# Tokens of each L1 run placed in four groups of two tiles instead of two groups of four, the slots of two groups computed together

## The chip, the cores and the metric

The kernel runs on one core of a Trainium2 chip. A core has engines that each work through their own instruction stream in order: TensorE (PE; the loading of its weights is listed as PEld), VectorE (DVE), ScalarE (ACT), GpSimd (POOL) and SyncE (SP, which here only starts DMAs). They wait for one another by semaphores. The metric is the device time of one execution in microseconds; the median of three runs counts.

## The reference

Two sequences of 1024 tokens with 256 features pass through six layers with residual sums. Everything is float32.

```python
x = x + 0.5 * _L0_ffn_ref(_layernorm(x), ...)     # MoE: 8 experts, top 2, width 176
x = x + _L0_attn_ref(_layernorm(x), ...)          # time mix and channel mix
x = x + 0.5 * _L0_ffn_ref(_layernorm(x), ...)
x = x + 0.5 * _L1_ffn_ref(_layernorm(x), ...)     # MoE: 32 experts, top 6, width 96
x = x + _L1_attn_ref(_layernorm(x), ...)          # linear attention: one sum over a sequence
x = x + 0.5 * _L1_ffn_ref(_layernorm(x), ...)
return x
```

The L1 mixture of experts takes a sigmoid of `x @ gate_w`, keeps the six highest of 32 scores, divides them by their sum, and adds up, with these weights, `silu(x @ wg[e]) * (x @ wu[e]) @ wd[e]` of the six experts; a shared expert of width 192 is added for every token. The attention's sum A runs over all tokens of one sequence, so its output exists only when all tokens of that sequence have been through it.

## The kernel before

The 2048 tokens are 16 tiles of 128, and they stay in SBUF as `x[0]` to `x[15]`. A mixture of experts is computed sparsely (`sparse_moe`): each pair of a token and a chosen expert gets a slot, a row of a DRAM tensor `xs`, so that blocks of 128 slots belong to one expert each. The steps of one such run are these.

- `prep`: normalize four tiles, transpose them, multiply with the router (`lg`), choose the experts (`route`: `taken` and the weights `comb`).
- `plan`: number the pairs. `count` sums up how many pairs each expert has, `cum` how many blocks it has opened, `rank` is a pair's place among its expert's pairs, and `far` holds, broadcast over the partitions, where an expert's blocks begin. From these come the slots and their six indices per token (`idx`). Blocks are numbered group by group: the tokens of a group fill the block that their expert has open, and then blocks opened for this group.
- `scatter`: one indirect DMA of GpSimd for each tile and each of the six choices writes the normalized rows to their slots in `xs` (line 566).
- `owners` finds which expert owns each block (`ends`, `passed`, `who`), `weights` the six factors of each token.
- `blocks`: for each block load 128 slots (`fetch`), transpose them (`px`), multiply with the gate and up weights of the block's expert (`pg`, L764), form the product `h` (L650), transpose it (`ph`), multiply with the down weights (`py`, L781), copy the result to `yb` (L789, VectorE) and store it to the DRAM tensor `ys`. An L1 run has 68 blocks that are always computed; 11 more lie behind a condition (`tc.If`, L906) that TensorE, VectorE, ScalarE and SyncE have to pass, and that borrow one buffer of the gathers.
- `gather` and `add_back` (`combine`): one indirect DMA of GpSimd for each tile and choice fetches result rows from `ys` (L801), and VectorE adds them, weighted, to `x` (L813). There are eight buffers `yk`, used in a ring.
- `shared`: the shared expert, tile by tile.

L1 has four such runs. Both sequences (A: tiles 0 to 7, B: tiles 8 to 15) go through the L1 mixture twice, with the attention between: 0A and 0B are the first passes, 1A and 1B the second (`m1` and `m2` in the code). The profile writes their names as L_0A, L_0B, L_1A and L_1B (xs_A, ys_A belong to both runs of A). The order on the chip is: blocks of 0A, blocks of 0B with the attention of A (`at`) between them, shared parts and the attention of B, blocks of 1A, blocks of 1B, and last the shared part of 1B with its gathers. Each run has two groups of four tiles, so 24 scatters and 24 gathers a group, 96 transfers a run.

A gather may read any block that can hold a pair of its group, so it waits for the stores of the first `first[g]` blocks, a bound that holds for any choice of experts:

```python
first = [moe_blocks(w, BT * (g + 1)) for g in range(NB)]   # L1: 55 and 79
```

The order of the work is made in two steps. While the program is written, a `Clock` with estimated costs (1.41 us for an L1 block, 1.27 us for a GpSimd call, 1.4 us for a pause) runs threads beside the main line of blocks: `between`, `first_pass`, `second_pass`, `sends` and `given_rows`. A thread waits for a condition (`0 in ready1[0]`), yields the time at which it wants to go on, and adds with `clock.spent` what its work costs the main line. A group's gathers begin when the main line has come to block `first[g]` + 3. After every third call on GpSimd stand five small memsets, a pause of the queue; in the last part pauses are off. Then a scheduler orders the instructions of each engine by a timeline of its own. The result is a fixed order on every engine: an instruction that waits holds all that stand behind it on its engine.

Of the kernel before, what the change touches and what calls it, by code (L numbers as in the profile page):

```python
# [8 lines left out]
F32 = mybir.dt.float32  # L9
I32 = mybir.dt.int32  # L10
AF = mybir.ActivationFunctionType
ALU = mybir.AluOpType
# [43 lines left out]
def macaron_kernel(ctx: ExitStack, tc: tile.TileContext, a: dict, out: bass.AP):  # L56
# [35 lines left out]

    before128 = const.tile([P, 32], F32, name="before128")
# [72 lines left out]
    def route(w, lg, name, taken=None, comb=None):  # L166
# [6 lines left out]
        s = small.tile([P, BT, S], F32, tag="s", name=f"s_{name}")  # L173
        nc.vector.memset(s, -1.0)
        sc = s[:, :, 0:E]
        if K == 2:
            mx = small.tile([P, BT], F32, tag="mx", name=f"mx_{name}")
            nc.vector.tensor_reduce(mx, lg, AX.X, ALU.max)
            nc.vector.tensor_tensor(
                sc, lg, mx.unsqueeze(2).to_broadcast([P, BT, E]), ALU.subtract  # L180
            )
            nc.scalar.activation(sc, sc, AF.Exp)
            tot = small.tile([P, BT], F32, tag="tot", name=f"tot_{name}")
# [3 lines left out]
                sc, sc, tot.unsqueeze(2).to_broadcast([P, BT, E]), ALU.mult  # L187
# [3 lines left out]
        m8 = small.tile([P, BT, 8], F32, tag="m8", name=f"m8_{name}")  # L191
        for i in range(BT):
            nc.vector.max(m8[:, i, :], s[:, i, 0:E])
# [3 lines left out]
        rest = small.tile([P, BT, S], F32, tag="rest", name=f"rest_{name}")  # L197
        for i in range(BT):
            nc.vector.match_replace(rest[:, i, :], m8[:, i, :], s[:, i, :], -2.0)
        if taken is None:  # L200
            taken = small.tile([P, BT, E], F32, tag="taken", name=f"taken_{name}")
        nc.vector.tensor_scalar(taken, rest[:, :, 0:E], -1.5, None, ALU.is_lt)
        if comb is None:
            comb = small.tile([P, BT, E], F32, tag="comb", name=f"comb_{name}")
# [3 lines left out]
        else:  # L208
            tot = small.tile([P, BT], F32, tag="tot", name=f"tot_{name}")
# [4 lines left out]
                comb, comb, tot.unsqueeze(2).to_broadcast([P, BT, E]), ALU.mult  # L214
# [180 lines left out]
    HT = NT // 2  # L395
    QK = 3
# [3 lines left out]
    def sparse_moe(layer, w, name, x, xs, ys, moe, given=None, out=None, bufs=2):  # L400
# [6 lines left out]
        NB = NT // BT  # L407
        NBLK, sure = moe_blocks(w, NT), SURE[layer]

        first = [moe_blocks(w, BT * (g + 1)) for g in range(NB)]  # L410
# [32 lines left out]
        def prep(b):  # L443
            sub = f"{name}_{b}"
            ts = slice(BT * b, BT * b + BT)
            xb, xbT, o = places(BT * b)
            xb = [xb[:, o + i, :] for i in range(BT)]
            sent[b] = xb
            features_of(b, xb, xbT, o, sub)
            lg = bank("pt", f"lg_{sub}")[:, 0 : BT * E].rearrange("p (t e) -> p t e", e=E)  # L450
            for i in range(BT):
                for c in range(DC):
                    nc.tensor.matmul(
                        lg[:, i, :],
                        xbT[:, c, (o + i) * P : (o + i + 1) * P],
# [4 lines left out]
            route(w, lg, sub, taken[:, ts, :], comb[:, ts, :])  # L460

        def plan(g):


            sub = f"{name}_{g}"
            lo, hi = BT * g, BT * g + BT
            pc = bank("pt", f"count_{sub}")
            for t in range(lo, hi):
                nc.tensor.matmul(
                    pc[0:E, 0:1], taken[:, t, :], ones, start=(t == lo), stop=(t == hi - 1)  # L470
                )


            count = small.tile([E, 1], F32, tag="count", name=f"count_{sub}", bufs=2)
            if g == 0:
                nc.vector.tensor_copy(count, pc[0:E, 0:1])
            else:
                nc.vector.tensor_tensor(count, pc[0:E, 0:1], groups[-1]["count"], ALU.add)
            over = small.tile([E, hi], F32, tag="over", name=f"over_{sub}")
            nc.vector.tensor_scalar(over, steps128[0:E, 0:hi], count, None, ALU.is_lt)  # L480
            cum = small.tile([E, 1], F32, tag="cum", name=f"cum_{sub}", bufs=5)
            nc.vector.tensor_reduce(cum, over, AX.X, ALU.add)
            own = cum
            if g > 0:
# [51 lines left out]
            else:  # L536

                def wide(v):
                    return v.unsqueeze(1).to_broadcast([P, BT, E])
# [1031 lines left out]
```

## Time and profile before

| | us |
|---|---|
| median of three runs | 1432.81 (1429.22 to 1433.11) |
| the profiled execution | 1429.86 |
| its span, first to last instruction | 1428.0 |
| TensorE busy | 1255.6 |
| GpSimd busy | 667.6 |

The span is read in stages. From the timelines: L0 lies before about 700; the blocks of 0A run from 731 to 855, those of 0B to 1041, those of 1A from 1156 to 1270, those of 1B to 1372. GpSimd's transfers lie as follows.

| GpSimd | from | to | number |
|---|---|---|---|
| scatters of 0A | 626.8 | 717.1 | 24 + 24, gathers of L0 between |
| scatters of 0B | 731.7 | 809.3 | 48 |
| gathers of 0A | 838.4 | 935.9 | 48 |
| gathers of 0B | 983.0 | 1093.8 | 24 + 24, 12 scatters of 1A between |
| scatters of 1A | 1021.1 | 1152.0 | 12 + 36 |
| scatters of 1B | 1152.3 | 1229.6 | 48 |
| gathers of 1A | 1251.8 | 1342.4 | 48 |
| gathers of 1B | 1354.4 | 1420.0 | 48 |

A view of waits names, for each instruction that began late, the engine and line whose semaphore came last. A timeline lists instructions with their start, their length and, in brackets, how long their engine stood idle before them and what ended that.

### The profile page before, as it was taken

What the parts mean: (1) busy time and instruction counts of PE and PEld (TensorE: products, weight loads), DVE (VectorE), ACT (ScalarE), POOL (GpSimd) and SP (SyncE); (2) the same over time, 40 slices, a digit from 0 to 9 for tenths busy, and PEclk for the clock granted to TensorE, in tenths of its full rate; (3) what the DMA queues carried; (4) which work ended last, traced back from release to release, by engine and by line L of the source; (5) the groups of instructions that cost most, each with busy time, mean ns of one, the idle gap of its engine ahead of it and who ended that gap; (6) DMA issues with size and microseconds to landing.
All of it is one profiled execution on the core that took longest, in us unless ns stands there. A gap on an engine that the chain in (4) does not pass through costs nothing. (4 is left out here: it accounts for less than half of the span.)

```text
span 1428.0 us, 23152 instructions
## 1 busy us (share of the span) xinstructions
PE 1255.6 (88%) x6100; PEld 973.0 (68%) x6100; DVE 737.3 (52%) x2507; ACT 631.9 (44%) x1671; POOL 667.6 (47%) x1346
## 2 busy tenths in 40 slices
PE   6599889889999789989979999988888789999970
PEld 4577657456666667757658987776665578988850
DVE  4433444865552432455536446665577446456653
ACT  4023562487674323362434555453333235555520
POOL 1640532010111460267777537413767777366475
PEclk8589889889999769989968999999879779999995
DMA  9723422990000922433476778443322247778843
GB/s 284 240 76 107 137 82 65 318 310 22 0 0 14 233 86 88 135 110 116 142 222 211 248 216 239 124 146 91 112 67 71 82 161 254 229 231 261 247 138 104
DMA packets 195170, 214.94 MB, mean 151 GB/s; under 512 B 40892, under 2 KB 178012, under 8 KB 195036
## 3 DMA queue, kind: packets, MB, share of 16 engines
q1 hardware_dynamic: 170460, 146.22, 33.2%
q0 software_dynamic: 24576, 67.14, 15.5%
q8 instruction: 59, 0.97, 0.3%
q14 instruction: 75, 0.61, 0.2%
HBM read 103.04 MB, written 110.23 MB: 149 GB/s over the span
## 5 line engine op out<-in xcount | busy, mean ns | idle before, releaser
L801 POOL DMA_INDIRECT yk_L<-ys_L,idx_L x64 | 62.1, 971 | 185.4 <-DMA ys_L<-yb_L 122.5
L333 POOL MEMSET still<- 128x96 f32 x628 | 112.7, 179 | 35.9
L764 PE MATMUL pg_L_b<-L0gu,xbT_L 128*128 x312 | 110.3, 479 | 0.0
L566 POOL DMA_INDIRECT xs_L<-xn_L,idx_L x64 | 61.9, 967 | 74.0 <-DVE idx_L L557 36.4
L659 PE MATMUL pg_L<-L0sgu,xTs_L 128*128 128x352 f32 x256 | 91.9, 495 | 2.8 <-DVE h_L L650 2.8
L801 POOL DMA_INDIRECT yk_L_0B<-ys_B,idx_L_0B x48 | 48.8, 1017 | 72.0 <-DMA ys_B<-yb_L_0B 47.0
L781 PE MATMUL py_L_b<-L0down,hT_L_b 88*128 x312 | 81.4, 383 | 0.0
L801 POOL DMA_INDIRECT yk_L_0A<-ys_A,idx_L_0A x48 | 46.6, 970 | 61.9 <-DMA xb_L_0A<-xs_A 29.2
L781 PEld LDWEIGHTS py_L_b<-L0down,hT_L_b 88*128 88x128 f32 x312 | 59.3, 193 | 19.7 <-issue 0.7
L764 PEld LDWEIGHTS pg_L_b<-L0gu,xbT_L 128*128 128x128 f32 x312 | 56.5, 199 | 20.1 <-issue 3.0
L650 DVE TENSOR_TENSOR h_L_b<-g_L_b,pg_L_b 128x176 f32<-128x176 f32 x78 | 26.2, 336 | 83.6 <-ACT g_L_b L649 73.7
L801 POOL DMA_INDIRECT yk_L_1A<-ys_A,idx_L_1A x48 | 46.3, 964 | 48.5 <-DMA xb_L_1A<-xs_A 22.2
L659 PEld LDWEIGHTS pg_L<-L0sgu,xTs_L 128*128 128x128 f32 x256 | 49.0, 204 | 27.0 <-DVE h_L L650 5.0
L983 PE MATMUL pkk_cm<-mk_cm,w_WkeyT 128*128 128x512 f32 x128 | 62.6, 621 | 4.9 <-DVE mk_cm L975 3.2
L764 PE MATMUL pg_L_0A_b<-L1gu,xbT_L_0A 128*128 x272 | 60.0, 347 | 1.8 <-DVE shift_L_0B L135 0.9
L764 PE MATMUL pg_L_0B_b<-L1gu,xbT_L_0B 128*128 x272 | 60.7, 350 | 0.8 <-DVEq L906 0.8
L801 POOL DMA_INDIRECT yk_L_1B<-ys_B,idx_L_1B x48 | 45.8, 954 | 27.2 <-DMA ys_B<-yb_L_1B 12.0
L995 PE MATMUL pkv_cm<-w_WvalT,sk_cm 128*128 128x256 f32 x256 | 58.0, 380 | 0.1
L764 PE MATMUL pg_L_1B_b<-L1gu,xbT_L_1B 128*128 x272 | 56.3, 329 | 1.6 <-DVEq L906 1.6
L764 PE MATMUL pg_L_1A_b<-L1gu,xbT_L_1A 128*128 x272 | 57.2, 334 | 0.5 <-DVE m_L_1B L194 0.4
L649 ACT ACTIVATE g_L_b<-pg_L_b 128x176 f32<-128x176 f32 x78 | 24.7, 317 | 72.6 <-PE pg_L_b L764 69.3
L995 PEld LDWEIGHTS pkv_cm<-w_WvalT,sk_cm 128*128 128x128 f32 x256 | 48.3, 190 | 12.0 <-issue 5.0
(639 smaller groups left out, 3387.5 us busy)
## 6 DMA issues: line engine op xcount, KB each, us to landing
xs_A<-zero SPq DMA_DIRECT2D x1, 10112.0 KB
xs_B<-zero SPq DMA_DIRECT2D x1, 10112.0 KB
xb_L<-xs_L SPq DMA_DIRECT2D x78, 128.0 KB
ys_L<-yb_L SPq DMA_DIRECT2D x78, 128.0 KB
xb_L_0A<-xs_A SPq DMA_DIRECT2D x68, 128.0 KB
ys_A<-yb_L_0A SPq DMA_DIRECT2D x68, 128.0 KB
xb_L_0B<-xs_B SPq DMA_DIRECT2D x68, 128.0 KB
ys_B<-yb_L_0B SPq DMA_DIRECT2D x68, 128.0 KB
```

The costliest lines, as they stand in the source:

```text
L333: d = nc.gpsimd.memset(still, 0.0)
L566: d = nc.gpsimd.indirect_dma_start(out=xs, out_offset=bass.IndirectOffsetOnAxis(ap=idx[:, t, k : k + 1], axis=0), in_=sent[g][t - BT * g], ...
L649: nc.scalar.activation(g, pg[:, 0:width], AF.Silu)
L650: nc.vector.tensor_tensor(dst, g, pg[:, width : 2 * width], ALU.mult)
L659: nc.tensor.matmul(pg, xbT[:, c, i * P : (i + 1) * P], w["sgu"][:, c, u, :, :].rearrange("p z w -> p (z w)"), start=(c == 0), stop=(c == D ...
L764: nc.tensor.matmul(pg, xbT[:, c, :], w["gu"][:, c, bass.ds(e, 1), :, :].rearrange("p e z h -> p (e z h)"), start=(c == 0), stop=(c == DC - 1),
L781: mm = nc.tensor.matmul(py, hT[0:HP, k, :], w["down"][:, bass.ds(e, 1), k, :].rearrange("p e d -> p (e d)"), start=(k == 0), stop=(k == C ...
L801: d = nc.gpsimd.indirect_dma_start(out=yk, out_offset=None, in_=ys[0 : n * P, :], in_offset=bass.IndirectOffsetOnAxis(ap=idx[:, t, k : k + ...
L983: nc.tensor.matmul(ps, w[:, c, oc * P : (oc + 1) * P], src[:, c, :], start=(c == 0), stop=(c == DC - 1),)
L995: nc.tensor.matmul(ps, src[:, c, i * P : (i + 1) * P], w[:, c, :], start=(c == 0), stop=(c == n - 1),)
```

## The change

The number of tiles in a group becomes a parameter `GT` of `sparse_moe`: four for L0 as before, two (`FINE`) for L1. An L1 run then has four groups, and `first` is 43, 55, 67 and 79. Slots are still planned for four tiles at a time, that is for two groups at once (`plan(g0, g1)`), so the same number of plans is made, but each has terms for two groups: the counts of both come from one chain of matmuls against shifted columns of a constant `ramp` (zeros and then ones), `cum` has a column for the state before, `far` has up to six parts instead of up to three, a pair that lies past the first group's open block gets a first shift and one past the second's a second (`more`), and the blocks left open (`open`) are worked out behind the indices. `owners` works with four group ends instead of two. Gathers, scatters and the threads count four groups; the attention starts when both groups of its four tiles have been added; the estimated cost of a plan goes from 3.5 (7.0) to 4.5 (8.0). The tiles `s`, `m8`, `rest` of `route` and `over` have one buffer instead of two.

```diff
+    ramp = const.tile([P, 2, BT], F32, name="ramp")
+    nc.gpsimd.memset(ramp[:, 0, :], 0.0)
+    nc.gpsimd.memset(ramp[:, 1, :], 1.0)
...
+    FINE = 2
...
-        first = [moe_blocks(w, BT * (g + 1)) for g in range(NB)]
+        first = [moe_blocks(w, GT * (g + 1)) for g in range(NG)]
...
-        def plan(g):
+        def plan(g0, g1):
...
             for t in range(lo, hi):
+                j = (t - lo) // GT
                 nc.tensor.matmul(
-                    pc[0:E, 0:1], taken[:, t, :], ones, start=(t == lo), stop=(t == hi - 1)
+                    pc[0:E, 0:G],
+                    taken[:, t, :],
+                    ramp[:, BT - j : BT - j + G],
+                    start=(t == lo),
+                    stop=(t == hi - 1),
                 )
...
+            cum = small.tile([E, 1 + G], F32, tag="cum", name=f"cum_{sub}", bufs=5)
+            if was is None:
+                nc.vector.memset(cum[:, 0:1], 0.0)
+            else:
+                nc.vector.tensor_copy(cum[:, 0:1], was["cum"])
+            nc.vector.tensor_reduce(cum[:, 1 : G + 1], over, AX.X, ALU.add)
+            own = small.tile([E, G], F32, tag="own", name=f"own_{sub}", bufs=2)
+            nc.vector.tensor_tensor(own, cum[:, 1 : G + 1], cum[:, 0:G], ALU.subtract)
...
+            shift0 = [(col(own, 0), before128)] if was is None else []
+            sums = [
+                ([(col(cum, j), others128)] if g0 + j else []) + [(col(own, j), before128)]
+                for j in range(G)
+            ]
+            sums += [[(col(cum, j), own128)] + shift0 for j in range(G) if g0 + j]
+            last = g1 == NG
+            if not last:
+                sums += [[(col(own, j), ident)] for j in range(G) if g0 + j]
...
+                for j in range(G - a):
+                    more = sl
+                    if j:
+                        more = small.tile([P, n, E], F32, tag="s", name=f"more_{sub}_{j}", bufs=1)
+                    nc.vector.tensor_tensor(more, pr, wide(far[:, G + j, :]), ALU.is_ge)
+                    nc.vector.tensor_tensor(more, more, wide(step[:, j, :]), ALU.mult)
+                    if j:
+                        nc.vector.tensor_tensor(sl, sl, more, ALU.add)
...
+            if not last:
+                for j in range(G - a):
+                    gone = small.tile([P, E], F32, tag="open", name=f"open_{sub}_{j}", bufs=2)
+                    nc.vector.tensor_tensor(gone, far[:, j + a, :], open_, ALU.subtract)
+                    nc.vector.scalar_tensor_tensor(
+                        gone, far[:, 2 * G - a + j, :], 0.5, gone, ALU.is_gt, ALU.mult
+                    )
+                    nc.vector.tensor_tensor(gone, gone, open_, ALU.add)
+                    open_ = gone
...
-            n = first[t // BT]
+            n = first[t // GT]
...
         for g in range(TPB // BT):
-            yield from wait(lambda: g in added)
+            yield from wait(lambda: {2 * g, 2 * g + 1} <= added)
...
+        n = m["groups"] // 2
         with behind_blocks():
-            m["plan"](g)
-        yield clock.spent(3.5, 7.0)
-        planned.add(g)
+            m["plan"](n * g, n * g + n)
+        yield clock.spent(4.5, 8.0)
+        planned.update(range(n * g, n * g + n))
...
     def sends(m, planned, sent, h, rank):
-        for g in range(2):
+        for g in range(BT):
             yield from wait(lambda: g in planned[h])
             yield from m[h]["scatter"](g, rank)
             sent[h].add(g)
```

In the fixed order that results, GpSimd has, between the gathers of run 0A and the last scatters of 1A: 24 gathers of 0B, 12 scatters of 1A, 12 gathers of 0B, 3 scatters, 12 gathers, 33 scatters. Before it had 23 gathers, 2 scatters, 1 gather, 10 scatters, 24 gathers, 36 scatters. Each L1 run has 42 matmuls instead of 29 in its counts, ranks, `far`, `ends` and `owners`, and 52 VectorE operations instead of 34 in its plans and owners.

## The prediction

> **What bounds the kernel now.** I read the page first, then the chain that ended last, TensorE's and GpSimd's busy time by stage, GpSimd's waits, and the timelines around those waits. On the page TensorE is the busiest engine:
>
> ```profile
> span 1428.0 us, 23152 instructions
> PE 1255.6 (88%) x6100; PEld 973.0 (68%) x6100; DVE 737.3 (52%) x2507; ACT 631.9 (44%) x1671; POOL 667.6 (47%) x1346
> ```
>
> But the shares hide stages with other limits. The busy time by stage (columns: stretch, its length, then PE, PEld, DVE, ACT, POOL busy, granted clock, DMA share, GB/s):
>
> ```profile
> 945.00:1045.00 100.00, 83.88 (x382) 66.30 (x383) 56.12 (x209) 40.05 (x104) 45.23 (x91) 0.83 0.30 95
> 1100.00:1165.00 65.00, 52.05 (x223) 41.27 (x222) 29.02 (x104) 20.07 (x45) 51.58 (x111) 0.74 0.30 103
> 1165.00:1260.00 95.00, 94.56 (x608) 85.53 (x608) 49.98 (x187) 50.39 (x192) 57.85 (x121) 1.00 0.73 232
> 1385.00:1428.00 43.00, 0.37 (x2) 0.00 (x0) 15.62 (x33) 0.00 (x0) 26.62 (x28) 0.55 0.37 107
> ```
>
> The expert blocks (1165 to 1260) are TensorE's: 94.56 of 95 us. The last 43 us are not: TensorE has nothing left, and the chain that ended last goes through GpSimd's gathers of run 1B, 1.25 us apart, to the last add. So in the tail the time at which the gathers begin decides. What they wait for (engine, line, releaser: us in all, times, longest):
>
> ```profile
> POOL yk_L_0B L801 <- DMA ys_B<-yb_L_0B: 47.0, 1, 47.0
> POOL yk_L_0A L801 <- DMA xb_L_0A<-xs_A: 29.2, 1, 29.2
> POOL yk_L_1A L801 <- DMA xb_L_1A<-xs_A: 22.2, 1, 22.2
> POOL yk_L_1B L801 <- DMA ys_B<-yb_L_1B: 12.0, 1, 12.0
> ```
>
> Once in each of the four L1 runs GpSimd stands idle until block 54 is stored. In the tail, on GpSimd's timeline:
>
> ```profile
> 1341.49 0.95 POOL L801 DMA_INDIRECT yk_L_1A<-ys_A,idx_L_1A  x1 [0.52 <-DVE h_L_1B_b L650]
> 1354.42 0.94 POOL L801 DMA_INDIRECT yk_L_1B<-ys_B,idx_L_1B  x1 [11.97 <-DMA ys_B<-yb_L_1B]
> ...
> 1419.03 0.94 POOL L801 DMA_INDIRECT yk_L_1B<-ys_B,idx_L_1B  x1 [0.30 <-DVE x L813]
> ```
>
> From 1354.42 on nothing holds it: 48 gathers, the first 11 in the paced rhythm (three, then five memsets, 5.1 us), the rest 1.25 us apart.
>
> In the middle, blocks of run 1A start when the last scatter of xs_A (1151.08 to 1152.04) has landed; on TensorE's timeline:
>
> ```profile
> 1149.69 2.39 PE L995 MATMUL po_at<-wA_at,axT_at 128*128 128x256 f32 x8
> 1155.84 1.12 PE L742 MATMUL px_L_1A<-ident,xb_L_1A 128*128 128x128 f32 x4 [3.76 <-DMA xb_L_1A<-xs_A]
> ```
>
> **The change, part by part.**
>
> *When gathers may start.* A group's gathers wait for as many blocks as can at most hold its pairs: (tiles x 768 + 4064)/128, now 43, 55, 67, 79 (before: 55 and 79). So 12 of 48 gathers may start after block 42 instead of 54.
>
> *The tail.* Copies of block results: block 42 ends at 1333.9, block 54 at 1350.5, and the first gather came 3.9 us after the latter. So run 1B's gathers start at 1337.8, if run 1A's are over: these also start 17 us earlier (1231.7 against 1248.7 for block 42 and 54 of 1A) and ended at 1342.4, so at about 1331 even with another 6 us of stalls. In the changed order of GpSimd five pauses lie in the first 15 gathers (before: four in the first 11). A pause adds 1.36 us to a gather's step. The 22nd gather would start at 1337.8 + 21 x 1.25 + 5 x 1.36 = 1370.9, but it takes a buffer that the conditional blocks (L906) hold until TensorE passes them (before it was the 19th):
>
> ```profile
> 1377.87 1.53 PE L659 MATMUL pg_L_1B<-L1sgu,axT_at 128*128 128x384 f32 x4 [0.81 <-DVEq L906]
> ```
>
> That place in TensorE's order is the same after the change. So the 22nd gather starts at 1378.2 and the 48th 26 x 1.25 later, 1410.7 instead of 1419.03: **-8.3**. Bounds: if the buffer comes free earlier, 1370.9 + 32.5 = 1403.4, -15.6; if the gathers hold the blocks up, half of it. I take the gate, since in run 1A the gather with that buffer stood 1.51 us until TensorE had passed.
>
> *More work for the slots.* Counted in the two instruction orders, a run gets 13 more small matmuls on TensorE (7 of L518, 4 of L590, 2 of L610) and 18 more operations on VectorE. From TensorE's timeline four L518 take 0.9 us (0.23 each), two L590 0.14, an L610 0.3: 7 x 0.23 + 4 x 0.07 + 2 x 0.3 = 2.5 us a run. VectorE: 0.07 to 0.47 us (L543 to L548, L605), 0.25 on average, 4.5 us a run; its share in those stages is at most 81% (44.57 of 55), and it costs only where TensorE waits for it. Run 0A and half of 0B lie beside the L0 blocks, where TensorE has few gaps (1.3 and 0.9 us) and the load of L1's down weights (702) waits for its end: 2.5 (0 to 3.7). The second half of 0B lies beside 0A's blocks: 1.4. So 0B's blocks start **+3.9** late (0 to 5). The second half of 1B beside 1A's blocks: 1.4; two output matmuls (po_at, 0.95 each) now stand behind 1A's first blocks, where they no longer fill the wait of 3.76: 1.0 (0 to 1.9). **+2.4**. L0's runs: one or two tiny operations more a group (0.07 to 0.15), while the update of the open blocks (0.3) moves behind idx: from -0.9 to +0.6, taken as 0. The scratch of route is single now, but all its users stand in one order on VectorE: 0 (to +1).
>
> *The middle.* The orders of VectorE and TensorE move attention A ahead: its first normalization from block 20 of run 0B to block 11, the second from 45 to 37, its output, 1A's router and slots in front of block 66. I walk along VectorE by the distances of before (without the 3.9). First normalization 889.5 -> 873.5; fourth tile 917.4 -> 901.4; 17 blocks of 1.49: second normalization 947.6 -> 933; block 42 stored 943, so gather 1 at 947 (before 983). Output and normalization for 1A 1001 -> 986; block 54 at 1000 (before 980), because pA, four po and the router now precede it. The second dozen of gathers runs 1004 to 1024; before they ran on by themselves. Their add-backs stand on VectorE in front of block 61's gate product and 1A's second normalization: 1021 + 3.9 = 1025. Behind these lie the router, the slots and blocks 61 to 66: block 66 copied at 1043 (before 1030.6), the last at 1048 (1041.2). GpSimd: 12 scatters 1024 to 1043, then the third dozen of gathers, which stands in front of all other scatters and waits for block 66: 1047 to 1067; 3 scatters to 1072; the last dozen to 1092; 33 scatters of 1.61 to 1145, with 3 us of stalls 1148 instead of 1152: **-4.0**. The bounds are wide: -12 if block 66 comes at 1038 and nothing stalls (before, the same 24 gathers took 2.03 each), +8 if block 66 comes 10 us later or add-backs stall as before.
>
> *Sum:* 1429.9 (the profiled execution; span 1428.0) + 3.9 - 4.0 + 2.4 - 8.3 = 1423.9. The median shown is 1432.81, 2.95 above it, so about **1427** for the median.
>
> [...] The row first: before 1A's first transposes TensorE stood 5.81 us, with only output matmuls ahead of it, and the granted clock was 0.83 in that stage; at the second such place shared matmuls stood between and the gap was 3.66. After the change the second place is bare too: by the rows 2.15 us more, which the walk along VectorE contains. [...]
>
> **The rivals.** (1) *More than that:* the buffer's gate doesn't bind in the tail. For it: before, the 19th gather had 0.30 us of idle time, no wait. Against: run 1A's 1.51. Tail -15.6 instead of -8.3: 1420 by the median, and with the middle's good end (-12) 1412. (2) *Slower:* one mechanism, in the middle: the third dozen of 0B's gathers stands in GpSimd's one queue in front of 1A's remaining scatters, and block 66 is late because attention's work is in front of it and its add-backs wait for the second dozen. Each us of lateness past 1047 passes to the start of 1A's blocks. It decides when the third dozen starts after about 1057: then +6 instead of -4 and 1437; at 1062, 1442. For it: the wait of 47.0 shows that these gathers hang on the blocks, and they are issued in order. Against: GpSimd has 26 us of slack before (from about 921 to 947) and a dozen done early. (3) *No change:* TensorE pays all of the extra matmuls (+7.3), the middle gives nothing and the tail -8.3: 1432. (4) *The change doesn't do what it says,* if GpSimd isn't free when block 42 is stored; in the tail it is, about 6 us before.
>
> **How the numbers follow.** Forecast 1427, own range 1421 to 1433: 0.42. Rival 1 (1412 to 1420): 0.24. Rival 2 (1437 to 1442): 0.20. Rival 3 (1430 to 1436): 0.14; rival 4 is under 0.01. A measurement tells about 0.3% (4.3 us) from no change, so faster means below 1428.5: 0.24 + 0.33 of the forecast's = 0.57. Slower means above 1437.1: 0.20 with rival 2's upper part and what I have not seen. The rest, 0.23, within. The range reaches from rival 1's good end to rival 2's middle: 1413 to 1439.
>
> **What would show it.** Run 1B's first gather at about 1338 minus the shift of the start, the 22nd held until TensorE passes L906's place, the last about 8 us sooner after that; run 0B's gathers in four dozens with a stop before the second (until block 54) and before the third (until block 66); xs_A's last scatter a few us sooner than 1152. The prediction is wrong if the third dozen starts far from 1047 + 4, or if the tail's gathers run without a stop.

## The result, and the profile after

The changed kernel took 1449.26 us (median, 1448.80 to 1457.41) beside 1431.01 us (1425.51 to 1433.11) of the kernel before, four runs of each: a ratio of 1.0144, 95% interval 1.0111 to 1.0178. The prediction was 1427, range 1413 to 1439, most likely faster. It was wrong in sign, and the time lies above the range.

The page of the changed kernel has 19 us more span, and TensorE is busy for 12 us more of it:

```profile
span 1447.0 us, 23428 instructions
PE 1267.9 (88%) x6200; PEld 985.2 (68%) x6200; DVE 751.0 (52%) x2593; ACT 625.1 (43%) x1667; POOL 667.3 (46%) x1353
```

The next view is the busy time by stage, in stretches shifted so that they lie at the same work as those shown of before (stretch, its length, PE, PEld, DVE, ACT, POOL, granted clock, DMA share, GB/s):

```profile
957.00:1057.00 100.00, 87.07 (x448) 69.64 (x447) 59.37 (x232) 37.65 (x104) 45.84 (x96) 0.83 0.33 102
1112.00:1177.00 65.00, 48.82 (x193) 38.20 (x194) 28.03 (x105) 13.90 (x34) 42.91 (x89) 0.66 0.24 83
1178.00:1273.00 95.00, 92.01 (x574) 82.29 (x574) 50.19 (x192) 49.01 (x172) 67.53 (x144) 0.95 0.70 219
1404.00:1447.00 43.00, 7.20 (x30) 5.00 (x30) 17.77 (x39) 1.56 (x5) 26.65 (x28) 0.63 0.37 107
```

In the second row, the stretch up to 1A's first blocks, the granted clock fell from 0.74 to 0.66 and GpSimd was busy for 42.91 us instead of 51.58. In the third, 1A's first blocks, it is 0.95 instead of 1.00. In the last row TensorE still has 7.20 us of work where before it had 0.37: the tail is now shorter than 43 us.

From the timelines of the two profiled executions, the sum of the change stage by stage ("block 0 of 0A" is the copy of its result on VectorE):

| stage | before | after | difference |
|---|---|---|---|
| start to L0's second scatters | 478.8 | 481.0 | +2.2 |
| to block 0 of 0A | 276.5 | 282.2 | +5.7 |
| to block 0 of 0B | 99.3 | 101.5 | +2.2 |
| to block 42 of 0B | 87.3 | 90.3 | +3.0 |
| to the last scatter of 1A | 210.1 | 209.2 | -0.9 |
| to block 0 of 1A | 16.2 | 17.5 | +1.3 |
| to block 15 of 1A | 25.2 | 38.6 | **+13.4** |
| to the last block of 1B | 178.5 | 177.1 | -1.4 |
| to the last gather of 1B | 48.1 | 41.6 | **-6.5** |
| sum | 1420.0 | 1439.0 | +19.0 |

The tail gave about what was forecast. The largest loss stands in a place to which the prediction gave 2.4 us: the first fifteen blocks of 1A. TensorE's timeline there, in the changed kernel:

```profile
1159.42 2.05 PE L1045 MATMUL po_at<-wA_at,axT_at 128*128 128x256 f32 x4
1167.91 0.69 PE L790 MATMUL px_L_1A<-ident,xb_L_1A 128*128 128x128 f32 x2 [6.43 <-DMA xb_L_1A<-xs_A]
1168.53 0.79 PE L531 MATMUL rank_L_1B<-before,own_L_1B 32*128 32x128 f32 x2
...
1171.11 0.61 PE L552 MATMUL far_L_1B<-ident,own_L_1B 32*128 32x32 f32 x2
...
1172.13 1.91 PE L1045 MATMUL po_at<-wA_at,axT_at 128*128 128x256 f32 x4
...
1176.97 1.89 PE L1045 MATMUL po_at<-wA_at,axT_at 128*128 128x256 f32 x8
...
1186.42 1.54 PE L161 MATMUL pt_L_1B<-ident,axl_at 128*128 128x128 f32 x8 [2.03 <-DVE axl_at L152]
1188.43 3.68 PE L461 MATMUL lg_L_1B<-L1router,axT_at 128*128 128x32 f32 x16 [0.46 <-ACT axT_at L443]
```

The same place in the kernel before, where the transposes of block 0 come at 1155.84:

```profile
1146.83 0.79 PE L502 MATMUL rank_L_1B<-before,cum_L_1B 32*128 32x128 f32 x2
1147.42 0.47 PE L518 MATMUL far_L_1B<-before,cum_L_1B 32*128 32x32 f32 x2
1147.82 4.26 PE L995 MATMUL po_at<-wA_at,axT_at 128*128 128x256 f32 x12
...
1163.41 1.87 PE L453 MATMUL lg_L_1B<-L1router,axT_at 128*128 128x32 f32 x16
```

(In these rows each matmul of the kernel counts twice, a transpose once: the router's x16 are eight matmuls, the x12 of `po_at` the outputs of three tiles.)

In the changed kernel the transposes of 1A's block 0 (L790) wait 6.43 us for the last scatter of 1A, and now the last part of `rank` and all of `far` of 1B's first plan, and the outputs of three of the four remaining tiles (`po_at`), stand behind them. Before, all of these stood in front. So work that was ready filled nothing, and 1B's slots came late. The rows of the next normalization, which need those outputs, came late too, and TensorE waits a second time for them (2.03 us). VectorE waits for `far`, and GpSimd for the indices (VectorE's timeline, then GpSimd's):

```profile
1171.76 0.29 DVE L561 COPY far_L_1B<-far_L_1B 128x128 f32<-128x128 f32 x1 [9.76 <-PE far_L_1B L552]
...
1174.49 0.17 DVE L593 TENSOR_SCALAR idx_L_1B<-top_L_1B 128x24 int32<-128x24 f32 x1
```

```profile
1163.24 0.96 POOL L614 DMA_INDIRECT xs_A<-axl_at,idx_L_1A  x1 [0.30 <-issue]
...
1174.93 0.96 POOL L614 DMA_INDIRECT xs_B<-axl_at,idx_L_1B  x1 [9.59 <-DVE idx_L_1B L593]
```

Before, on VectorE's timeline, 1B's indices were written two microseconds ahead of 1A's last scatter (1151.08):

```profile
1148.79 0.18 DVE L557 TENSOR_SCALAR idx_L_1B<-top_L_1B 128x24 int32<-128x24 f32 x1
```

In the tail, GpSimd's timeline shows the earlier start and a stop:

```profile
1363.64 0.94 POOL L849 DMA_INDIRECT yk_L_1B<-ys_B,idx_L_1B  x1 [3.72 <-DMA xb_L_1B<-xs_B]
...
1392.94 0.95 POOL L849 DMA_INDIRECT yk_L_1B<-ys_B,idx_L_1B  x1 [0.30 <-DVE h_L_1B L698]
1402.71 1.06 POOL L849 DMA_INDIRECT yk_L_1B<-ys_B,idx_L_1B  x1 [8.82 <-DVE x L861]
...
1438.01 0.94 POOL L849 DMA_INDIRECT yk_L_1B<-ys_B,idx_L_1B  x1 [0.30 <-DVE x L861]
```

19 gathers run, the twentieth stands for 8.82 us until an add-back of VectorE (L861) has been done, and the last 29 run 1.25 us apart.

### The profile page after: what moved, and what is told of

Read it like the earlier page. It is cut to its first block, busy times and chain, and to the rows that moved or that the text cites. A ratio compares the mean times of both kernels' runs of the same rounds, so it can differ in the third digit from the quotient of the medians.

```text
span 1447.0 us, 23428 instructions
## 1 busy us (share of the span) xinstructions
PE 1267.9 (88%) x6200; PEld 985.2 (68%) x6200; DVE 751.0 (52%) x2593; ACT 625.1 (43%) x1667; POOL 667.3 (46%) x1353
## 5 line engine op out<-in xcount | busy, mean ns | idle before, releaser
L698 DVE TENSOR_TENSOR h_L_b<-g_L_b,pg_L_b 128x176 f32<-128x176 f32 x78 | 26.2, 336 | 86.8 <-ACT g_L_b L697 74.2
L707 PEld LDWEIGHTS pg_L<-L0sgu,xTs_L 128*128 128x128 f32 x256 | 47.7, 199 | 25.2 <-DVE h_L L698 4.4
L614 POOL DMA_INDIRECT xs_B<-axl_at,idx_L_1B x48 | 46.6, 971 | 23.6 <-issue 11.9
```

Of the source, the lines that this page charges most:

```text
L614: d = nc.gpsimd.indirect_dma_start(out=xs, out_offset=bass.IndirectOffsetOnAxis(ap=idx[:, t, k : k + 1], axis=0), in_=sent[t], in_offset=None,
L698: nc.vector.tensor_tensor(dst, g, pg[:, width : 2 * width], ALU.mult)
L707: nc.tensor.matmul(pg, xbT[:, c, i * P : (i + 1) * P], w["sgu"][:, c, u, :, :].rearrange("p z w -> p (z w)"), start=(c == 0), stop=(c == D ...
```

## The experiments

The theory after the result: the order of TensorE at 1A's head costs most of it. The rivals: GpSimd's line of gathers in front of 1A's scatters (the prediction's rival 2), and the longer slot computation itself. The kernel before took between 1427 and 1458 us on different chips and at different times, so kernels are compared by their ratios to the runs of before that were made beside them. In the names, `px` means that 1A's first block is pinned as in the first experiment, `fine` which L1 runs have two-tile groups while the others have four-tile ones, `np` that GpSimd's pauses end earlier. All of them compute the whole result.

### The order at 1A's head

**px_last.** The changed kernel, in which 1A's blocks are written down after 1B's first plan, and block 0's transposes may only be issued behind `far` and the last output matmul.

```diff
-    settle(lambda: BT - 1 in sent2[0])
+    settle(lambda: BT - 1 in sent2[0], lambda: 0 in ready2[1])
...
+            with ExitStack() as st:
+                if name == "L1_1A" and b == 0:
+                    for v in (pe_mark["far"], pe_mark["at_1", 7]):
+                        st.enter_context(tc.issue_after(v))
+                for c in range(DC):
                     nc.tensor.transpose(
```

> The changed kernel, with one thing forced: 1A's first block transposes (line 790) may not stand on TensorE in front of 1B's first slot matmuls (L531, L552) and the last attention output matmul (po_at_1_7, L1045). Theory 1, TensorE's order at the head of 1A: the first fifteen blocks of 1A took 13.4 us longer after the change because the transposes wait for the last scatter with 1B's slots queued behind them; here they take about 25 us again and the time falls by 9 to 14 us, to 1435-1440. Theory 2, GpSimd's head of the line: the loss stands in the late third dozen of gathers, the order of TensorE costs nothing, and the time stays at 1447-1451. Theory 3, the slot computation of two groups at once is dear wherever it stands: at most 3 us come back, 1446-1449.

Measured: 1466.82 us, 1.0070 of before (1.0044 to 1.0095). The first fifteen blocks took 31.7 us, and GpSimd went from 1A's last scatter to 1B's first in 4.0 us instead of 10.7. The changed kernel stood at 1.0144, and at 1.0116 when it was run again (after_again below); by these ratios 0.5 to 0.7% come back, 7 to 11 us, half of the loss or a little less. Expected were 9 to 14 us.

**before_px_first.** The kernel before with that order: 1B's first plan is written down after 1A's first block step, and its last `rank` matmul is forced behind the transposes. The second normalization's transposes went behind block 5 with it, as in the changed kernel.

```diff
             planning.append(m)
+            if m is m2.get(1):
+                yield from wait(lambda: ("L1_1A", 1) in steps_done)
...
+            with ExitStack() as st:
+                if name == "L1_1B" and g == 0:
+                    st.enter_context(tc.issue_after(pe_mark["L1_1A", 0].ins))
                 nc.tensor.matmul(
                     pr,
                     more.to_broadcast([E, P]),
```

> The kernel before, with the order of TensorE at 1A's first block made like that of the changed one: 1B's first plan is written down after 1A's first block step and its last rank matmul is forced behind the block's transposes. Groups, gathers and scatters are those of before. Theory 1: the order alone costs 8 to 13 us, 1439-1444. Theories 2 and 3: it costs at most 2 us, 1430-1433.

Measured: 1465.64 us, 1.0053 (1.0032 to 1.0074), so about 7.7 us (4.7 to 10.8) for the order alone, with nothing else of the change. The first fifteen blocks took 38.9 us.

**old_consts** and **old_consts_px.** The change raised the planner's cost of a plan. These two put it back, without and with the pin; the instructions are those of the changed kernel, in another order.

```diff
-        yield clock.spent(4.5, 8.0)
+        yield clock.spent(3.5, 7.0)
```

> The changed kernel with the planner's cost of a plan back at 3.5 (7.0), which is a change of the order alone: the instructions and their data are the same. At 0A's head TensorE's order becomes nearly that of before (block 2 in front of 0B's second normalization, the first output of a block in front of 0B's group ends); at 1A's head the first transposes stay in front of 1B's slots. If the order at 0A's head is what makes 0A's first block come 6 to 8 us late (it did in all six profiles with fine 0A and 0B): it comes at 753 to 758, and the time is 4 to 8 us under the changed kernel, 1.008 to 1.011 of before. If it is the longer slot computation itself: no change, 1.012 to 1.015.

> The one above with 1A's first block pinned behind 1B's first slots and the last attention output matmul. Beside it on the same chip it gives the price of the order at 1A's head directly: by the traces 9 to 13 us (first fifteen blocks of 1A in 25 to 32 us instead of 38 to 42). If both orders are what costs: 0.998 to 1.003 of before. If only that at 1A's head: 1.004 to 1.008.

Measured on one chip: 1451.40 us, 1.0180 (1.0155 to 1.0204), without the pin, and 1435.94 us, 1.0068 (1.0046 to 1.0091), with it. This pair gives the price of the order in these kernels: 15.5 us. The ratio of old_consts lies above both ranges that were expected for it. The two stand one above the other in TensorE's timeline, first old_consts, then old_consts_px:

```profile
1162.78 1.20 PE L790 MATMUL px_L_1A<-ident,xb_L_1A 128*128 128x128 f32 x4 [8.57 <-DMA xb_L_1A<-xs_A]
1163.91 0.79 PE L531 MATMUL rank_L_1B<-before,own_L_1B 32*128 32x128 f32 x2
...
1183.93 1.37 PE L161 MATMUL pt_L_1B<-ident,axl_at 128*128 128x128 f32 x8 [2.90 <-DVE axl_at L152]
1185.76 3.69 PE L461 MATMUL lg_L_1B<-L1router,axT_at 128*128 128x32 f32 x16 [0.46 <-ACT axT_at L443]
```

```profile
1158.52 0.79 PE L532 MATMUL rank_L_1B<-before,own_L_1B 32*128 32x128 f32 x2
...
1161.64 4.98 PE L1051 MATMUL po_at<-wA_at,axT_at 128*128 128x256 f32 x12
1166.46 0.60 PE L796 MATMUL px_L_1A<-ident,xb_L_1A 128*128 128x128 f32 x4
...
1172.08 1.04 PE L161 MATMUL pt_L_1B<-ident,axl_at 128*128 128x128 f32 x8
...
1174.04 1.88 PE L462 MATMUL lg_L_1B<-L1router,axT_at 128*128 128x32 f32 x16
```

With the slots and output matmuls in front, the wait of 8.57 us is gone altogether, they fill it, and the same router matmuls take 1.88 us instead of 3.69: the granted clock is 1.00 there (1173 to 1183 below). The busy time by stage says the same (first old_consts, then old_consts_px; the clock is the third column from the right):

```profile
1160.00:1170.00 10.00, 7.22 (x28) 6.51 (x29) 2.48 (x15) 2.65 (x5) 0.00 (x0) 0.50 0.29 93
1170.00:1180.00 10.00, 10.00 (x59) 9.18 (x58) 3.10 (x9) 5.18 (x16) 7.86 (x17) 0.95 0.51 163
1180.00:1190.00 10.00, 6.51 (x31) 5.15 (x29) 4.14 (x19) 4.68 (x9) 8.00 (x17) 0.73 0.46 154
```

```profile
1163.00:1173.00 10.00, 7.93 (x41) 6.59 (x40) 5.53 (x23) 5.93 (x13) 6.28 (x13) 0.85 0.53 172
1173.00:1183.00 10.00, 9.51 (x76) 8.46 (x73) 4.30 (x29) 6.04 (x14) 7.88 (x19) 1.00 0.53 167
```

In all five profiles with the transposes in front the first fifteen blocks took 38.5 to 42.1 us, in the fifteen others 24.6 to 33.1.

How the order turned over can be read in part from the planner's own clock. Before, it wrote down 1B's first plan at 717.24 and 1A's first transposes at 722.43. In the changed kernel, 1B's router came 7 us later on that clock (712.24 instead of 705.24), so the plan stood at 724.24, and the transposes at 723.93: 0.31 us in front. But the scheduler that follows has a say too: with 1A's first block written down after the plan, and no pin, it still puts the transposes in front of the last part of `rank`; so those 0.31 us alone do not explain the order. Nor is it the raised cost alone: with the old one, 1B's router is planned at 705.24 as before, but 1A's scatters are planned to end earlier, its transposes come at 715.93, and they stay in front.

In old_consts the first block of 0A came 277.2 us after L0's second scatters, in place of the 282 to 285 of the six profiles with fine 0A and 0B and the new cost; so that delay is one of order. But the time was not better for it: 1.0180, beside 1.0116 to 1.0144 of the changed kernel.

### The rewriting without finer groups

**coarse.** The changed kernel with `GT` four in all L1 runs; the threads count two groups again.

```diff
-    FINE = 2
+    FINE = {(0, 0): 4, (0, 1): 4, (1, 0): 4, (1, 1): 4}
+    GS = {k: HT // v for k, v in FINE.items()}
```

> The changed kernel with four-tile groups in all four L1 runs: the rewritten slot computation, the single-buffered scratch tiles and the planner's costs of 4.5/8.0 are in it, the finer placing and the earlier gathers are not. Theory 1 and theory 2: no loss without the fine groups, within 3 us of before, 1429-1434, and TensorE's order at 1A's head is that of before. Theory 3 in its form that the rewriting itself costs (scratch tiles, constants): 1436-1442.

Measured: 1454.64 us, 0.9973 (0.9951 to 0.9996). The rewritten slot computation, the single buffers and the planner's raised cost lose nothing by themselves.

### What is left in front

**after_again** is the changed kernel unaltered, beside the next two.

> The changed kernel unaltered, beside the same runs of before as the three that follow, so that the parts are compared with the whole on one chip. 1.4% above before, as in the first comparison.

Measured: 1470.13 us, 1.0116 (1.0076 to 1.0155). L0's second scatters began at 478.9 here: the first 2.2 us of the table above do not belong to the change.

**fine_0A_px**, **fine_0B_px**, **fine_0AB_px.** As coarse, with two-tile groups in 0A, in 0B and in both, and the pin.

```diff
+    FINE = {(0, 0): 2, (0, 1): 4, (1, 0): 4, (1, 1): 4}   # 0A; 0B has (0, 1): 2
```

> Two-tile groups in 0A alone, 1A's first block pinned behind 1B's first slots. It holds the costs that the traces show up to 0B's first block: 0B's second plan in front of 0A's first outputs, and 0A's gathers brought forward. If the +10 us that stand at 0B's first block after the change come from 0A's own fine groups and reach the end: 8 to 12 us above before. If they are taken up by the waits of the middle (the third dozen of gathers sets 1A's start whatever came before): within 3 us of before.

> Two-tile groups in 0B alone, 1A's first block pinned. It holds the middle of the change: 0B's first gathers brought forward, the first attention half in front of 0B's blocks 54 to 66, the third dozen of gathers in front of 1A's remaining scatters. The prediction's rival 2: block 66 comes late, the third dozen with it, and 1A's last scatter 8 us or more later than before: 6 to 12 us above before. The prediction's own step: the last scatter of 1A comes 4 us earlier: 2 to 6 us below before.

> Two-tile groups in 0A and 0B, four-tile groups in 1A and 1B, 1A's first block pinned: the part of the change in front, without the tail's. 0A alone stood at 1.0048 and 0B alone at 1.0034 of before, four-tile groups in all runs at 0.997. If the two add: 1.010 to 1.014. If they are one loss (GpSimd's and the blocks' turn in the middle) that either brings: 1.004 to 1.008.

Measured: 1459.68 us, 1.0048 (1.0020 to 1.0075), 7 us; 1457.31 us, 1.0034 (1.0014 to 1.0055); 1440.78 us, 1.0074 (1.0048 to 1.0101). The last lies in the range that was expected if 0A and 0B are one loss (1.004 to 1.008) and below that for two that add (1.010 to 1.014, counted from the 0.997 of coarse). Counted from before, 0.48 and 0.34% would add up to about the 0.74 measured; the intervals do not decide between the two. Together they are as much as is left of the loss once the order at 1A's head is mended (1.0070 and 1.0068); but those two kernels have the shorter tail as well, so this is no full account. The expectation for fine_0B_px put the attention half in front of 0B's blocks into the wrong run: it is 0A's gathers that bring it there. In fine_0A_px the blocks 42 to 54 of 0B took 50.5 us, in fine_0B_px 39.3, before 38.1. The first two runs lie outside their own ranges: fine_0A_px was expected 8 to 12 us above before or within 3, fine_0B_px 6 to 12 above or 2 to 6 below.

A longer first plan can be read directly. From L0's second scatters to 0A's first scatter, all profiles with four-tile groups in 0A (late_px, whose L0 gathers were moved, left out) have 148.1 to 149.2 us, all with two-tile groups 151.1 to 151.2. VectorE's timeline of fine_0B_px (one group in 0A's first plan) and then of the changed kernel (two):

```profile
622.58 0.14 DVE L498 COPY count_L_0A<-count_L_0A 32x1 f32<-32x1 f32 x1
...
626.09 0.17 DVE L596 TENSOR_SCALAR idx_L_0A<-top_L_0A 128x24 int32<-128x24 f32 x1
```

```profile
625.26 0.14 DVE L496 COPY count_L_0A<-count_L_0A 32x2 f32<-32x2 f32 x1
...
631.62 0.18 DVE L593 TENSOR_SCALAR idx_L_0A<-top_L_0A 128x24 int32<-128x24 f32 x1
```

From `count` to `idx` it is 3.5 us with one group and 6.4 with two. But these 2.9 us do not reach the blocks: in fine_0A_px the first block of 0A came 276.5 us after L0's second scatters, and 0B's first block 378.3, beside 275.6 and 378.0 in fine_1AB_px on the same chip. What is late in fine_0A_px lies behind: from 0B's first block to 1A's last scatter it is 310.5 us, beside 300.1 in fine_1AB_px and in fine_0B_px, the blocks 42 to 54 above all; some 4.5 us of it are made up again before 1A's first block.

**late_px** and **late1_px.** px_last, with the gathers of a pair of groups released together, so that nothing is read earlier than before. In late_px the edit reached L0's blocks too, whose gathers of the second run began at 605.0 instead of about 590; its 1452.83 us (1.0151, 1.0104 to 1.0198) tell nothing of the question. late1_px keeps L0 as it was.

```diff
-            n = first[t // GT]
+            n = first[t // GT | (layer == "L1")]
...
-                if g < NG and q == first[g] + 3:
-                    ready.add(g)
-                    g += 1
+                if g < NG and q == first[g | (layer == "L1")] + 3:
+                    ready.update((g, g | (layer == "L1")))
+                    g = (g | (layer == "L1")) + 1
```

> Two-tile groups in all four L1 runs, 1A's first block pinned, but gathers released as before: a group's rows are read only when the pair of groups (four tiles) is ready, so tokens are placed in fine groups and nothing is read earlier. If the loss in front of 1A is due to the planner writing the attention halves and 1A's plans in front of 0B's last blocks because the gathers come earlier: the loss in front is gone, the tail's gain too, and the time is within 4 us of before. If it is due to the longer slot computation: it stays, 8 to 14 us above before.

> As late_px, with the release of gathers in pairs held to the four L1 runs (in late_px the edit also reached L0's blocks, whose gathers came 13 us later, so that it settled nothing). Fine placing is kept, nothing of L1 is read earlier than before, 1A's first block is pinned. If early reading brings both the loss in front and the tail's gain: 0.998 to 1.004 of before. If the longer slot computation carries the loss in front by itself: 1.008 to 1.016.

Measured for late1_px: 1446.11 us, 1.0116 (1.0061 to 1.0172). Fine placing loses in front without any early reading, and without early reading the tail gains nothing (48.2 us). So early reading is not what causes the loss in front, as the first branch had it. The ratio lies in the range of the second branch, the longer slot computation (1.008 to 1.016); no run shows by which wait that would reach the end. How 0A's and 0B's share comes about is not settled, and the slot computation of two groups stays a rival for it.

### The tail

The time from 1B's last block to the end of its last gather, by the runs that have two-tile groups:

| fine runs | profiles | us |
|---|---|---|
| neither 1A nor 1B | before, coarse, before_px_first, fine_0A_px, fine_0B_px, fine_0AB_px | 48.1 to 51.4 |
| all four, read late | late_px, late1_px | 48.1 and 48.2 |
| 1B alone | fine_1B_px | 48.3 |
| 1A and 1B | changed kernel (twice), px_last, old_consts and _px, after_xb, fine_1AB_px, fine_1AB_xb | 38.9 to 44.3 |
| neither, pauses ended early | before_np | 44.2 |
| 1A and 1B, pauses ended early | fine_1AB_np, fine_1AB_xb_np | 33.7 and 34.0 |

**fine_1B_px** and **fine_1AB_px**: `FINE` is 2 for 1B alone, and for 1A and 1B, with the pin.

> Two-tile groups in 1B alone, four-tile groups in the other three runs, and 1A's first block forced behind 1B's first slots and po_at_1_7. What is left of the change is the tail: 1B's gathers may start after the second group of tiles' blocks instead of after all of the first half's. The prediction's term for the tail was -8.3 us, the traces of before and after show about -6.4 between the last block and the end. If the tail's gain is real and stands alone: 1423-1428. If it comes only because the blocks were late in the changed kernel: 1430-1434. Theory 3 would have one costly plan (1B's) beside 1A's scatters and end at 1431-1436.

> Two-tile groups in 1A and 1B, four-tile groups in 0A and 0B, 1A's first block pinned. In the runs so far the stretch from 1B's last block to the last gather was 41 to 42 us where 1A and 1B were both fine, and 48 to 50 us where 1A was coarse, whether 1B was fine or not: GpSimd, still at 1A's gathers, did not use 1B's earlier readiness. If that is the reason, the tail's 7 to 9 us come back here with nothing lost in front: 5 to 9 us below before. If the earlier end of 1A's gathers was owed to the late blocks of the changed kernel: within 3 us of before.

Measured: 1458.79 us, 1.0013 (0.9982 to 1.0045); 1449.20 us, 0.9980 (0.9960 to 1.0000). With 1B alone GpSimd is at 1A's gathers until 1368.2 and cannot use the earlier release; with 1A's gathers early too, the tail is 40.5 us. The mean over the eight profiles of the fourth row is 41.2, over the nine of the first three 49.2: 8 us, as forecast. The time does not show this gain, though: fine_1AB_px was expected 5 to 9 us below before and stands at 0.9980, beside 0.9973 of coarse, which has no pin; and px_last and old_consts_px, with the shorter tail, stand no lower than fine_0AB_px without it.

**after_xb** and **fine_1AB_xb**: the conditional blocks of 1B take their input from the blocks' ring and not from that of the gathers.

```diff
-            for k, kind in (("xb", "spare"), ...
+            for k, kind in (("xb", "xb" if name == "L1_1B" else "spare"), ...
```

> The changed kernel with one buffer moved: the conditional blocks of 1B take their input tile from the blocks' own ring of five instead of from the ring of eight that the gathers use. The prediction said that in the tail a gather of 1B is held until TensorE has passed the conditional blocks, because they hold one of the gathers' buffers; in the changed kernel the twentieth gather stood from 1393.9 to 1402.7. If that buffer is what holds it: the stop goes, the 20th to 36th gathers run on, and the time falls by 6 to 9 us against the changed kernel. If the stop is the conditional branch itself, which GpSimd passes too: no change within 3 us.

> Two-tile groups in 1A and 1B alone, 1A's first block pinned, and the conditional blocks' input tile out of the gathers' ring as above. Fine 1A and 1B alone stood at 0.998 of before. If the buffer holds the gathers: 0.990 to 0.995 of before. If not: 0.996 to 1.000.

Measured: 1450.36 us, 1.0138 (1.0099 to 1.0177); 1427.46 us, 1.0002 (0.9974 to 1.0029). No change. In after_xb's timeline of GpSimd the stop is still there, one gather later:

```profile
1398.77 0.94 POOL L849 DMA_INDIRECT yk_L_1B<-ys_B,idx_L_1B  x1 [0.30 <-issue]
1406.89 1.07 POOL L849 DMA_INDIRECT yk_L_1B<-ys_B,idx_L_1B  x1 [7.17 <-DVE x L861]
```

The releaser is an add-back (L861), which has to read its rows before their buffer can be filled again. On VectorE's timeline of the same kernel:

```profile
1405.17 0.35 DVE L698 TENSOR_TENSOR h_L_1B<-g_L_1B,pg_L_1B 128x192 f32<-128x192 f32 x1 [1.45 <-ACT g_L_1B L697]
1405.67 0.42 DVE L756 SCALAR_TENSOR_TENSOR x<-py_L_1B,x 128x256 f32<-128x256 f32 x1
1406.13 1.00 DVE L861 SCALAR_TENSOR_TENSOR x<-yk_L_1B,wk_L_1B,x 128x256 f32<-128x256 f32 x2
```

The add stands in VectorE's order behind the products of the shared expert (L698), each of which waits for ScalarE (the last five ahead of it in the changed kernel 0.93 to 1.45 us). In both kernels it is the thirteenth add-back of 1B: it ends at 1402.44 in the changed kernel and at 1406.62 in after_xb, and the gather that stands starts 0.27 us later. With one of the eight buffers lent to the conditional blocks the twentieth gather takes over the thirteenth's buffer, with none lent the twenty-first. The stop was predicted; the conditional blocks' buffer was not what makes it.

**fine_1AB_xb_np**, **before_np** and **fine_1AB_np**: GpSimd's pauses end at 1B's block step 43 instead of after its blocks.

```diff
             at_step["q"] = q + 1
+            if name == "L1_1B" and q == 43:
+                pauses["on"] = False
```

> As the one above, and the pauses of GpSimd (five memsets after every third transfer, 1.1 us and a fresh start of 0.5 us) left out from 1B's first ready group on. In the tail a gather takes 1.25 us without and about 1.7 us with pauses; some twenty-four gathers of 1B lie in the part with pauses. If GpSimd alone sets the tail: another 6 to 10 us, 0.984 to 0.990 of before. If the pauses give VectorE and the block loads their time: the blocks of 1B run later and the gain is gone, 0.992 to 1.000.

> The kernel before, with GpSimd's pauses left out from 1B's 43rd block step on, and nothing else. If the pauses alone hold the tail: 0.992 to 0.996 of before, as much as with fine groups in 1A and 1B. If the gathers must also be released earlier for it to matter (before, the second half of 1B's gathers waits for all blocks): 0.997 to 1.001.

> Two-tile groups in 1A and 1B, 1A's first block pinned, no pauses from 1B's 43rd block step on, the conditional blocks' input tile in the gathers' ring as before. With the tile moved, this stood at 0.9947 of before. The tile changed nothing measurable, so 0.992 to 0.998 is expected; it is faster than the kernel before without pauses by 3 us or more if the finer groups bring anything of their own.

Measured: 1421.27 us, 0.9947 (0.9922 to 0.9972); 1431.20 us, 0.9996 (0.9968 to 1.0024); 1423.66 us, 0.9967 (0.9940 to 0.9994). The kernel before gains nothing measurable from it. With fine 1A and 1B, both forms are faster than the kernel before: fine_1AB_xb_np 6.2 us below fine_1AB_xb on one chip, fine_1AB_np 7.5 us below before_np on another. So the best of what was measured is two-tile groups in the second passes alone, 1A's first block behind 1B's first slots, and no pauses once gathers of 1B may run. Whether the finer groups are needed for it is not fully shown: coarse alone stands at 0.9973, its interval overlaps with both, and coarse with the pauses ended early was not run.

## Why the prediction was wrong

The prediction's terms add up to -6.0 us, the pair of profiles shows +19.0. Of the 25 us between them, 10.9 lie in 1A's and 1B's blocks (+13.3 instead of +2.4, the rows from 1A's last scatter to 1B's last block), 6.1 in the middle (+2.1 instead of -4.0), 4.0 in front of 0B's blocks (+7.9 instead of +3.9), 1.8 in the tail, and 2.2 in front of L0's second scatters.

- **"Two output matmuls (po_at, 0.95 each) now stand behind 1A's first blocks ...: 1.0 (0 to 1.9)", and with it the +2.4.** This is the step that failed. The move was seen and two matmuls counted. What else stood behind the same wait was not: a third output, the last of `rank` and the six `far` matmuls of 1B's first plan, which decide 1B's indices, the next rows' normalization, and a second stop of TensorE. Measured: +13.4 us in the first fifteen blocks, 15.5 us of time between the two orders on one chip, 7.7 us when the kernel before gets that order.
- **"0B's blocks start +3.9 late."** +10.1 in the profiled pair, of which 2.2 were not the change's. That 0A's first plan takes 2.9 us longer does not confirm the term of 2.5, which was the time of the added matmuls of 0A and half of 0B on TensorE; and it is not seen at 0A's first block in fine_0A_px. The pair shows 5.7 us up to 0A's first block, of which five are gone in old_consts, with the order that the planner's old cost gives, but without gain in time. As a price in the time, 0A and 0B together cost 0.7% (0.5 to 1.0), 11 us; how is not settled.
- **The middle, -4.0.** From block 42 of 0B to the last scatter the walk had -5.1 and the pair shows -0.9; over seven profiles with early reading in 0A and 0B the stretch is 201 to 209 us, over nine with four-tile groups in both 210 to 216. So the walk had the direction of this stretch, with profiles of different chips. From 0B's first block to block 42 it had +1.1 and got +3.0.
- **The tail, -8.3.** -6.5 in the pair and -8 over the profiles, as a stretch of the profile and not as a gain in the time. The mechanism stands, with two corrections: it needs fine groups in 1A as well, and the gathers are held by an add-back that stands late on VectorE (8.82 us in the changed kernel, 7.17 in after_xb) and not by the conditional blocks' buffer (the twentieth, where the prediction had the 22nd); that the size came out so near is in part luck.
- **Rival 2** came nearest in sign and size (1437 to 1442), and its condition was met: the third dozen started at 1058.5, after 1057. But that is not what cost the time. The dozen was late because everything in front of 0B's block 42 was 13 us late; the stretch in which rival 2 puts its loss grew by nothing. **Rival 1** did not occur: the stop in the tail is there. **Rival 3**'s sum (1432) was not met either; the longer slot computation that it prices is still open as a part of what 0A and 0B cost. The change does what it says.
- **The stops in front of 1A's router, and the clock.** For the second stop the prediction had 2.15 us more. It was 5.34 us where it had been 3.67, the first 2.28 where it had been 5.81, and the granted clock of that stage is 0.83 in both profiles. Where the two kernels differ in the clock is another place, 1A's head. Read in 1-us windows, in the changed kernel it is 0.50 from 1150 to 1176, through the first stop, 1.00 from 1177 to 1186, and 0.50 again from 1187, behind the second stop. Before, it falls within the stop of 3.76 us (0.55 from 1154 to 1155), is 0.50 up to 1160, and 1.00 from 1161 on (the first blocks' products, L764, took 1.64 and 1.49 us at 1157 and 1159, and 0.81 at 1168). So blocks of 1A ran at 0.50 behind the first stop before the change as well; the fall behind the second is new.

## What to carry to other kernels

When an instruction that waits for a late transfer moves forward on an in-order engine, list everything that now stands behind it and who waits for that, not only its own kind; the price is the chain behind the wait, not the busy time of what moved. The order that comes out of a planner and a scheduler has to be read at each such place after an edit, and a place that must not turn over is better pinned. A change that acts in several stages is worth splitting by stage: here the same edit lost in the first passes and at 1A's head, and shortened the tail.

## What the hardware showed unexpectedly

The router matmuls of 1B's second four tiles (x16 in the rows), which lie among 1A's first blocks, took 1.87 to 1.88 us in the kernel before, px_last and old_consts_px, and 3.68 to 3.69 in the changed kernel, old_consts and before_px_first. Read in 1-us windows from 1100 to 1300, in the kernel before and in the changed one, the granted clock is 0.50 or 1.00, but for the windows in which it changes (0.53 to 0.98); so the 0.74, 0.66 and 0.95 of the stages are means over stretches at 0.50 and at 1.00. In the changed kernel it went from 1.00 to 0.50 around a wait of TensorE of 2.03 us; in old_consts_px it stayed at 1.00 (1170 to 1175) through a wait of 1.83 us among the same blocks.

On the changed kernel's timeline the last block matmul before the wait of 2.03 us ends at 1183.2 and the router begins at 1188.4, with transposes alone between; the granted clock is 1.00 up to 1186, 0.95 from 1186 to 1187, and 0.50 after that. What brought it down is not shown.

Times of one kernel moved by more than this change is worth: the kernel before took 1451.88 us and, at another time on the same chip, 1427.23. Only ratios to runs made beside each other could be compared.
